# Step orders of their own for the first three and the last four periods of a software-pipelined FP32 transformer kernel

## The chip, the cores and the metric

One core of one Trainium2 chip. The metric is the device time of one execution in microseconds (us), where lower is better. Every run quoted here was in the fast state, and all kernels gave correct results. PE is TensorE, PEld its weight loads, DVE VectorE, ACT ScalarE, POOL GpSimd and SP SyncE, which issues the large DMA transfers.

## The reference

128 batch items of S = 128 tokens with E = 512 features go through two layers, all in FP32: attention with 8 heads, whose scores are multiplied by twice the adjacency matrix, then a graph attention layer. Both are pre-normalised and residual.

```python
h = jnp.maximum(_layernorm(x, axis=-1), 0.0)
# layer 0
q, k, v = (proj(Wq, bq), proj(Wk, bk), proj(Wv, bv))         # proj: x @ W.T + b, 8 heads
scores = jnp.einsum('bhqd,bhkd->bhqk', q, k) * SCALE * (adj + adj)[:, None]
ctx = jnp.einsum('bhqk,bhkd->bhqd', softmax(scores), v)
x = x + jnp.einsum('bse,fe->bsf', ctx, Wo) + bo
# layer 1
h = jnp.maximum(_layernorm(x, axis=-1), 0.0)
Wh = h @ W
e = leaky_relu(Wh @ a[:512] + swapaxes(Wh @ a[512:], 1, 2), 0.2)
attention = softmax(where(adj > 0.5, e, -9e15), axis=1)
x = x + elu(attention @ Wh)
```

## The kernel before

The items are worked in N = 64 pairs, two pairs making a group. A 512x512 product is made from seven products of quarters (as in Strassen's method), some with *sums* of quarters of the weights (`weight_sums`, four additions on DVE) or of the activations (`hidden_sum`, four additions per group). A group has 21 such products (v0 to v6, q0 to q6, k0 to k6). Each is 4 matmuls, which the trace lists as 8 records of 128x256. Their results stand in PSUM banks "a", "b" and "c". ACT copies out the first one of a quadrant ("firsts"), DVE adds the others ("adds").

```python
SEQ = "v0 v1 v2 v3 v4 q0 v5 q1 v6 q2 q3 q4 k0 q5 k1 q6 k2 k3 k4 k5 k6".split()
N = B // 2                                                    # 64 pairs

def weight_sums(w):
    nc.vector.tensor_tensor(w[:, 4], w[:, 1], w[:, 0], OP.subtract)
    nc.vector.tensor_tensor(w[:, 5], w[:, 3], w[:, 4], OP.subtract)
    nc.vector.tensor_tensor(w[:, 1], w[:, 3], w[:, 1], OP.subtract)
    nc.vector.tensor_tensor(w[:, 6], w[:, 2], w[:, 5], OP.subtract)
```

All work of a pair is cut into steps with short names, and one list, `ORDER`, says in which order they are written in one period: "U4:0" is step U4 of this period's pair, "fb:4" step fb of the pair four before. There is no scheduler behind it (`manual_schedule`): the list is each engine's program. The names used below: U1 to U11 the products of the *next* group (U1 to U10 with the even pair of a group, the rest of SEQ with the odd one), F their firsts, A their adds, sca/scb the scores of a pair's two items, at, mx, ex, rc, nm their weighing and softmax, fl, bl, pl the transposition of the attention (on DVE, then through DRAM), pc the context product, o0 to o6 the output products of layer 0, d00 to d11 the dot products of layer 1, g its gather, w0 to w6 its output products, fa, fb, so the finish and the store.

Group 0 has no earlier pair that it could stand beside. It is straight-line code, and what is needed once hangs on the first use, as whole calls:

```python
    with tc.manual_schedule():
        ...                                # stats and transposes of pairs 0 and 1
        weight_sums(wv_sb)
        ...
        for n, u in enumerate(SEQ):
            firsts, adds = product(0, u[0], int(u[1]))
            if n == 2:
                weight_sums(wq_sb)
            ...                            # stats of pairs 2 and 3, sums of wk, sums of group 1
            firsts()
            adds()
        ...
        first_use = {
            (0, "mxa"): constant_c, (0, "mxb"): lambda: weight_sums(wo_sb), (0, "atb"): constant_u,
            (0, "st0"): spread_u, (1, "mxa"): lambda: weight_sums(w1_sb),
        }
        for p in range(early, N + late):   # -22 .. 91: periods at both ends are partly empty
            for step, lag in ORDER:
                pair = p - lag
                for do in tables.get(pair, {}).get(step), first_use.get((pair, step)):
                    if do:
                        do()
```

`constant_u` is eight dot products on DVE in one piece. At the end the periods simply run empty: there is no next group, so the U steps are missing and the rest stays in the same order.

Of the kernel before, what the change touches and what calls it, by code (L numbers as in the profile page):

```python
# [13 lines left out]
P = 128  # L14
# [10 lines left out]
def kernel(  # L25
# [40 lines left out]
    def load_x(p):  # L66

        xs[p] = io.tile([P, 2, E], F32, name="x")
        if p < 2:
            for i in range(2):  # L70
                nc.sync.dma_start(xs[p][:, i, :], x[2 * p + i])
        else:
            nc.sync.dma_start(xs[p], both(x, p))
# [6 lines left out]
    def half_of_hidden(p):  # L80

        g, i = divmod(p, 2)
        if i == 0:
            hAs[g] = grp.tile([P, 4, 2, 2 * S], F32, name="hA")
        return hAs[g][:, 2 * i : 2 * i + 2].rearrange("p q c k -> p (q c) k")

# [10 lines left out]
        adjTs[p] = aio.tile([P, 2, S], F32, name="adjT")  # L97
        nc.sync.dma_start(adjTs[p], both(adjT, p))

    load_x(0)  # L100
    load_x(1)

    ident = const.tile([P, P], F32, name="ident")
    make_identity(nc, ident)
    mhalf = const.tile([P, 1], F32, name="mhalf")
    nc.gpsimd.memset(mhalf, -0.5)

    def quarters(src, name):

        w = const.tile([P, 7, 2, E // 2], F32, name=name)  # L110
        nc.sync.dma_start(w[:, 0:4], src)
        return w

    def column(src, name):
        b = const.tile([P, C], F32, name=name)
# [1 line left out]
            nc.scalar.dma_start(b, src.rearrange("(c p) -> p c", p=P))  # L117
        return b

    def row(src, offset, name):  # L120
        b = const.tile([P, E], F32, name=name)
        nc.sync.dma_start(b, bass.AP(tensor=src.tensor, offset=src.offset + offset, ap=[[0, P], [1, E]]))
        return b

    bq_sb = column(bq, "bq")
    bk_sb = column(bk, "bk")
    bv_sb = column(bv, "bv")
    wv_sb = quarters(wvT, "wv")
    wq_sb = quarters(wqT, "wq")
    load_x(2)  # L130
    load_x0(3)
    wk_sb = quarters(wkT, "wk")
    load_adj(0)
    wo_sb = quarters(woT, "wo")
    c_sb = row(bo, 0, "c")
    w1_sb = quarters(w1, "w1")
    us_sb = row(a1, 0, "u_src")
    ut_sb = row(a1, E, "u_dst")



# [4 lines left out]
    FIRSTS = {0: (0, 0), 2: (1, 0), 4: (1, 1), 5: (0, 1)}  # L146
    ADDS = {1: (0, 0, "b"), 4: (1, 1, "c"), 6: (1, 0, "c")}

    def weight_sums(w):
        nc.vector.tensor_tensor(w[:, 4], w[:, 1], w[:, 0], OP.subtract)  # L150
        nc.vector.tensor_tensor(w[:, 5], w[:, 3], w[:, 4], OP.subtract)
        nc.vector.tensor_tensor(w[:, 1], w[:, 3], w[:, 1], OP.subtract)
        nc.vector.tensor_tensor(w[:, 6], w[:, 2], w[:, 5], OP.subtract)

    def token_sum(h, s, k):

# [22 lines left out]
        return mv, stats, power  # L179

    st0, rows0, qks, vs, scs, ats, trs, blocks, aTs, pcs = ({} for _ in range(10))
    l1s, h1s, wts, pbs, pgs, gTs, zs, ezs, posts = ({} for _ in range(9))

    def stats0(p, i, src=None):
        if p not in st0:
            st0[p] = row_stats(x0s.pop(p) if src is None else src, "mv0")
        st0[p][1](i)

    def hidden_T(p, src, tag):

        mv, _, power = st0.pop(p)
        power()
        dst = half_of_hidden(p)
        hn = work.tile([P, 2, E], F32, name="hn", tag=tag)
        for i in range(2):
            nc.vector.tensor_scalar(
                hn[:, i, :], src[:, i, :], mv[:, i, 0:1], mv[:, i, 1:2], op0=OP.subtract, op1=OP.mult
            )
        for i in range(2):
            pt = ps1.tile([P, C, P], F32, name="pt", tag="ps1")  # L200
            for c in range(C):
                nc.tensor.transpose(pt[:, c, :], hn[:, i, c * P : (c + 1) * P], ident)  # L202
            nc.scalar.activation(dst[:, :, i * S : (i + 1) * S], pt, AF.Relu)

    def spread0(p):

        mv, _, power = st0.pop(p)
        power()
        rows0[p] = dram.tile([2, P, 2], F32, name="rows0")
        with nc.allow_non_contiguous_dma(reason="two numbers of a row"):  # L210
            nc.gpsimd.dma_start(rows0[p].rearrange("b p s -> p b s"), mv)
# [285 lines left out]

    ucol = const.tile([P, 2, C], F32, name="ucol")

    def constant_c():  # L500

        pm = ps1.tile([P, 2, E // 2], F32, name="pm", tag="ps1")
        for f in range(2):
            for c in range(C):
                nc.tensor.matmul(
                    pm[:, f, :], bv_sb[:, c : c + 1].to_broadcast([P, P]), wo_sb[:, 2 * (c // 2) + f, c % 2, :],
                    start=(c == 0), stop=(c == C - 1),
                )
        nc.vector.scalar_tensor_tensor(c_sb, pm.rearrange("p f k -> p (f k)"), -1.0, c_sb, op0=OP.add, op1=OP.add)

    def constant_u():

        junk = work.tile([P, E], F32, name="junk")
        for i, u in ((0, us_sb), (1, ut_sb)):
            for c in range(C):
                k = c // 2
                nc.vector.scalar_tensor_tensor(  # L517
                    junk.rearrange("p (f k) -> p f k", f=2), w1_sb[:, 2 * k : 2 * k + 2, c % 2, :], 1.0,
                    u.rearrange("p (f k) -> p f k", f=2), op0=OP.mult, op1=OP.mult, accum_out=ucol[:, i, c : c + 1],
                )  # L520

    def spread_u():

        for i, u in ((0, us_sb), (1, ut_sb)):
            pu = ps1.tile([P, C, P], F32, name="pu", tag="ps1")
            for c in range(C):
                nc.tensor.transpose(pu[:, c, :], ucol[:, i, c : c + 1].to_broadcast([P, P]), ident)
            nc.scalar.activation(u, pu.rearrange("p c k -> p (c k)"), AF.Copy, scale=1.0 if i else 1.0 / MASK)


    SEQ = "v0 v1 v2 v3 v4 q0 v5 q1 v6 q2 q3 q4 k0 q5 k1 q6 k2 k3 k4 k5 k6".split()
# [1 line left out]



    ORDER = [
        (step.split(":")[0], int(step.split(":")[1]))
        for step in """
        F4:1 F6:1 flb:1 fb:4 U9:1 F9:1 g1:3 od5:2 ge1:3 o6:2 la:1 st0:2 s0:1 hd0:1 od6:2 U8:1 w0:3 st1:2 gs0:3 blb:1
        hd1:1 pw:2 w1:3 gs1:3 nm:2 U10:1 zc0:3 so:4 U1:0 gs2:3 h20:2 A9:1 A8:1 l0:0 wd1:3 w2:3 F10:1 gs3:3 h21:2 plb:1  # L540
        lx:1 hs0:1 zc2:3 lT:0 sca:0 pca:1 pcb:1 scb:0 w4:3 d00:2 d01:2 pea:1 A6:1 ata:0 mxa:0 peb:1 d10:2 w3:3 F1:0
# [2 lines left out]
        zc5:3 atb:0 F2:0 mxb:0 F3:0 o2:1 e1:2 A10:16 cs3:1 wd6:3 U5:0 F5:0 sw:2 exb0:0 A2:0 U4:0 exb2:0 A3:28 exb3:0  # L544
        exb1:0 A5:0 A11:1 bla:0 o3:1 rcb1:0 od2:1 nmb2:0 U6:0 hs3:1 o4:1 lt:0 rcb0:0 nmb0:0 t0:0 nmb3:0 nmb1:0 pla:0
        U7:0 ez:3 F7:0 F11:-22 g0:2 fa:3 od4:1 A1:15 od4c:1 ge0:2 o5:1 A7:14
        """.split()
    ]

    def steps(p):  # L550

        a, b = 2 * p, 2 * p + 1
        table = {}
        for s, n in (("a", a), ("b", b)):
            table |= {
                "sc" + s: lambda n=n: scores(n),
                "at" + s: lambda n=n: weigh(n),
                "mx" + s: lambda n=n: maxima(n),
                "fl" + s: lambda n=n: flip_blocks(n),
                "bl" + s: lambda n=n: send_blocks(n),  # L560
                "pl" + s: lambda n=n: place_blocks(n),
                "pc" + s: lambda n=n: context(n),
                "pe" + s: lambda n=n: keep_context(n),
            }
            for k in range(4):
                table[f"ex{s}{k}"] = lambda n=n, k=k: exps(n, k)
                table[f"nm{s}{k}"] = lambda n=n, k=k: normalise(n, k)
            for k in range(2):
                table[f"rc{s}{k}"] = lambda n=n, k=k: shares(n, k)
# [23 lines left out]
            "ez": lambda: elu(p), "fa": lambda: finish_a(p), "fb": lambda: finish_b(p), "so": lambda: store(p),  # L593
            "sh": lambda: shift(p),
        }
        if p > 2:
            table["lx"] = lambda: load_x(p)
        if p + 1 < N:
            table["la"] = lambda: load_adj(p + 1)
        if p + 4 < N:  # L600
# [22 lines left out]
        return table  # L623

    with tc.manual_schedule():
        def first_stats(p):
            stats0(p, 0, rows[p])
            stats0(p, 1)

        rows = [xs[0], xs[1], xs[2], x0s[3]]  # L630
        first_stats(0)
        first_stats(1)
        hidden_T(0, rows[0], "h2")
        hidden_T(1, rows[1], "z")
        weight_sums(wv_sb)
        for k in range(4):
            hidden_sum(0, k)
        for n, u in enumerate(SEQ):
            firsts, adds = product(0, u[0], int(u[1]))
            if n == 2:  # L640
                weight_sums(wq_sb)
            if n == 4:
                first_stats(2)
            if n == 6:
                hidden_T(2, rows[2], "h2")
            if n == 8:
                weight_sums(wk_sb)
            if n == 10:
                first_stats(3)
            if n == 12:  # L650
                hidden_T(3, rows[3], "z")
                load_x0(4)
            if n == 14:
                for k in range(4):
                    hidden_sum(1, k)
            firsts()
            adds()
        stats0(4, 0)
        stats0(4, 1)
        spread0(4)  # L660

        early, late = min(lag for _, lag in ORDER), max(lag for _, lag in ORDER)
        tables = {p: steps(p) for p in range(N)}

        first_use = {
            (0, "mxa"): constant_c, (0, "mxb"): lambda: weight_sums(wo_sb), (0, "atb"): constant_u,
            (0, "st0"): spread_u, (1, "mxa"): lambda: weight_sums(w1_sb),
        }
        for p in range(early, N + late):
            for step, lag in ORDER:  # L670
                pair = p - lag
                for do in tables.get(pair, {}).get(step), first_use.get((pair, step)):
                    if do:
                        do()


# [40 lines left out]
```

## Time and profile before

| | before |
|---|---|
| device time, median of 3 | 2416.63 us (2416.42 to 2416.77) |
| span of the profiled execution | 2412.4 us |
| PE busy / idle in it | 2366.6 / 45.8 us |

To read it: PE is the bound, so only two things can shorten the span. One is PE's *idle* time, 45.8 us. The other is the *slow* part of its busy time: the granted clock (the share of TensorE's full speed that it is allowed to run at) falls to half after some gaps, and the same matmuls are then busy for longer. The number of PE records is the same in every kernel below except two, where it is told. So less busy time means less work at half clock. The views are in the prediction.

### The profile page before, as it was taken

What the parts mean: (1) busy time and instruction counts of PE and PEld (TensorE: products, weight loads), DVE (VectorE), ACT (ScalarE), POOL (GpSimd) and SP (SyncE); (2) the same over time, 40 slices, a digit from 0 to 9 for tenths busy, and PEclk for the clock granted to TensorE, in tenths of its full rate; (3) what the DMA queues carried; (4) which work ended last, traced back from release to release, by engine and by line L of the source; (5) the groups of instructions that cost most, each with busy time, mean ns of one, the idle gap of its engine ahead of it and who ended that gap; (6) DMA issues with size and microseconds to landing.
All of it is one profiled execution on the core that took longest, in us unless ns stands there. A gap on an engine that the chain in (4) does not pass through costs nothing.

```text
span 2412.4 us, 40507 instructions
## 1 busy us (share of the span) xinstructions
PE 2366.6 (98%) x14264; PEld 2072.9 (86%) x14264; DVE 1993.3 (83%) x3909; ACT 1460.3 (61%) x4811; POOL 265.7 (11%) x323
## 2 busy tenths in 40 slices
PE   8899999999999999999999999999999999999987
PEld 7788888888888888888888888888888888888875
DVE  5788888888888888888888888888888888888776
ACT  2565666665666665656655656656666656666664
POOL 1011111111101101111111111111011011010000
PEclk9999999999999999999999999999999999999998
DMA  4434534544434545445445345455345454454232
GB/s 164 114 106 127 147 112 124 157 114 136 134 114 134 148 122 138 113 124 146 133 127 146 104 121 158 115 135 138 113 131 158 114 136 124 120 138 133 82 106 72
DMA packets 255275, 306.10 MB, mean 127 GB/s; under 512 B 21856, under 2 KB 181600, under 8 KB 254432
## 3 DMA queue, kind: packets, MB, share of 16 engines
q1 hardware_dynamic: 251568, 303.37, 45.0%
q8 instruction: 113, 1.85, 0.3%
q0 software_dynamic: 1920, 0.13, 0.2%
q14 instruction: 90, 0.74, 0.1%
q10 hardware_dynamic: 1584, 0.01, 0.0%
HBM read 202.64 MB, written 100.79 MB: 126 GB/s over the span
## 4 chain that ended last, share of the span: by engine, by line
PE 96%; DVE 2%; ACT 1%; DMA 1%; issue 0%; SPq 0%; POOL 0%; POOLq 0%; ACTq 0%; DVEq 0%
PE acc_a L261 27%; PE row_a L302 23%; PE acc_c L261 13%; PE row_c L302 9%; PE acc_b L261 7%; PE sc L323 6%; PE pc L386 5%; PE pg L464 5%; PE pb L432 1%; ACT at L341 0%; ACT at L350 0%; PE pt L202 0%; DVE junk L517 0%; DVE tr L357 0%; DVE at L329 0%
## 5 line engine op out<-in xcount | busy, mean ns | idle before, releaser
L341 ACT ACTIVATE at<-at,nmx 128x128 f32<-128x128 f32 x1024 | 397.1, 393 | 17.4 <-DVE nmx L336 16.4
L302 PE MATMUL row_a<-w,gT 128*128 128x256 f32 x1280 | 326.1, 385 | 7.7 <-DVE z L482 6.8
L302 PE MATMUL row_a<-wo,cxT 128*128 128x256 f32 x1280 | 322.3, 383 | 9.3 <-DVE x L400 9.3
L350 ACT ACTIVATE at<-at,rs 128x128 f32<-128x128 f32 x1024 | 316.5, 389 | 13.7 <-DVE rs L345 13.7
L176 POOL TENSOR_SCALAR mv<-mv 128x2 f32<-128x2 f32 x128 | 78.4, 613 | 2090.7 <-DVE mv L173 2090.7
L302 PEld LDWEIGHTS row_a<-w,gT 128*128 128x128 f32 x1280 | 237.9, 190 | 47.4 <-DVE z L482 8.4
L478 ACT COPY z<-row_a 128x256 f32<-128x256 f32 x256 | 92.8, 362 | 305.2 <-PE row_a L302 305.1
L302 PEld LDWEIGHTS row_a<-wo,cxT 128*128 128x128 f32 x1280 | 235.6, 192 | 37.3 <-DVE x L400 10.1
L329 DVE SCALAR_TENSOR_TENSOR at<-sc,adj 128x1024 f32<-128x1024 f32 x128 | 156.7, 1225 | 94.8 <-PE sc L323 92.6
L278 ACT ACTIVATE kT<-acc_a,bk 128x256 f32<-128x256 f32 x256 | 107.5, 471 | 162.2 <-PE acc_a L261 162.2
L341 ACT ACTIVATION_READ_ACCUMULATOR at<-at,nmx 128x1 f32 x1024 | 195.8, 191 | 0.0
L357 DVE STREAM_TRANSPOSE tr<-at 128x1024 f32<-128x1024 f32 x128 | 158.7, 1240 | 38.2 <-ACT at L350 37.5
L172 DVE BATCH_NORM_STATS2 st<-x 128x6 f32<-128x512 f32 x256 | 175.2, 685 | 8.8 <-DMA x<-in_x 4.3
L400 DVE TENSOR_TENSOR x<-row_a,x 128x256 f32<-128x256 f32 x320 | 132.6, 414 | 48.0 <-PE row_a L302 45.6
L273 ACT COPY v<-acc_a 128x512 f32<-128x512 f32 x128 | 74.8, 585 | 154.5 <-PE acc_a L261 154.5
L336 DVE TENSOR_REDUCE nmx<-at 128x8 f32<-128x1024 f32 x128 | 156.2, 1220 | 4.4
L393 ACT COPY cxT<-pc 128x512 f32<-128x512 f32 x128 | 75.0, 586 | 136.5 <-PE pc L386 136.5
L323 PEld LDWEIGHTS sc<-kT,qT 64*128 64x128 f32 x2048 | 125.6, 189 | 33.5 <-issue 31.8
L323 PE MATMUL sc<-kT,qT 64*128 64x128 f32 x2048 | 150.3, 287 | 1.3 <-DVE at L329 1.3
L464 PEld LDWEIGHTS pg<-w,h 128*128 128x128 f32 x1024 | 136.2, 194 | 8.6 <-ACT w L452 1.8
L177 POOL TENSOR_TENSOR mv<-mv,mhalf 128x2 f32<-128x2 f32 x128 | 140.6, 1099 | 10.7
L464 PE MATMUL pg<-w,h 128*128 128x128 f32 x1024 | 136.6, 277 | 1.4 <-DVE w L458 1.4
(126 smaller groups left out, 4995.0 us busy)
## 6 DMA issues: line engine op xcount, KB each, us to landing
blocks<-tr SPq DMA_DIRECT2D x128, 512.0 KB, 4.6
aT<-blocks SPq DMA_DIRECT2D x512, 128.0 KB, 3.0
x<-in_x SPq DMA_DIRECT2D x123, 512.0 KB, 5.3
out<-x SPq DMA_DIRECT2D x64, 512.0 KB, 5.0
hA<-in_xT SPq DMA_DIRECT2D x120, 256.0 KB, 4.5
mr<-rows SPq DMA_DIRECT2D x60, 256.0 KB, 5.0
adj<-in_adj SPq DMA_DIRECT2D x64, 128.0 KB, 2.9
adjT<-in_adjT SPq DMA_DIRECT2D x64, 128.0 KB, 3.4
```

Of the source, the lines that this page charges most:

```text
L172: nc.vector.bn_stats(st, src[:, i, :])
L177: nc.gpsimd.tensor_tensor(mv[:, :, 1], mv[:, :, 1], mhalf.to_broadcast([P, 2]), OP.pow)
L261: nc.tensor.matmul(acc[:, m, :], lhsT, rhs, start=fresh and m == 0 and c == 0, stop=c == 1, skip_group_check=True)
L302: nc.tensor.matmul(acc, left[:, la, c, :], w[:, wb, c, :], start=n in (0, 3) and c == 0, stop=c == 1, skip_group_check=True)
L323: nc.tensor.matmul(sc[:, s * C + j, :], qT[r, j, cols], kT[r, j, cols], start=True, stop=True)
L329: nc.vector.scalar_tensor_tensor(at, scs.pop(b), QSCALE, adjs[p][:, i : i + 1, :].to_broadcast([P, H, S]), op0=OP.mult, op1=OP.mult)
L336: nc.vector.tensor_reduce(nmx, at, AX.X, OP.max, negate=True)
L341: nc.scalar.activation(at[:, j, :], at[:, j, :], AF.Exp, bias=nmx[:, j : j + 1], accum_out=sums[:, j : j + 1])
L350: nc.scalar.activation(at[:, j, :], at[:, j, :], AF.Copy, scale=rs[:, j : j + 1])
L357: nc.vector.transpose(trs[b], at.rearrange("p h (j k) -> p j h k", k=Q))
L400: nc.vector.tensor_tensor(d, row_acc(p, "o", bank), d, OP.add)
L464: nc.tensor.matmul(pg[:, c, :], h1s[p][0][:, i, c * P : (c + 1) * P], wts[p][:, i, :], start=True, stop=True)
```

## The change

The intent is to fill the two ends. The middle list stays, but only for periods 3 to 59. Two explicit lists take the rest: `HEAD` (group 0 with the loads, the weights' sums and the periods 0 to 2) and `TAIL` (the last four periods, pairs counted from the end). For this, what were whole calls become single steps: `W{v,q,k,o,w}{0..3}` for the weights' sums, `cu00` to `cu11` for the dot products of `constant_u`, `sup`, `sua`, `ccp`, `ccd` for the other constants, `L...` for loads. No arithmetic comes or goes.

```diff
-    def weight_sums(w):
+    def weight_sum(w, k):
         ...                                        # one of the four subtractions
-    def constant_u():
+    def dots_u(i, half):                           # two of the eight dot products
+    HEAD = """
+        lx@0 t0@-5 Lu0@0 t1@-5 lt@0 Lq@0 Lk@0 pp@0 lx@1 hn0@0 hn1@0 tp0@0 Wq0@0 Lu1@0 t1@-4 t0@-4 tp1@0 pp@1 Wq2@0 hn0@1
+        ev0@0 Lv@0 ev1@0 U3@-1 U5@-1 Wk0@0 U1@-2 lx@2 hn1@1 F1@-2 tp1@1 Lo@0 tp0@1 Wq1@0 la@-1 Lw@0 ev0@1 la@0 ev1@1
+        ...                                        # 372 steps in all
+    """
     ORDER = ...                                    # unchanged
+    TAIL = """
+        ...
+        U2@-4 nma2@-2 pcb@-3 m1@-5 scb@-2 st0@-4 pea@-3 od6@-4 st1@-4 fla@-2 e1@-5 A9@-3 so@-6 sw@-5 peb@-3 o0@-3 g1@-5
+        ...                                        # 598 steps in all
+    """
-        first_use = { ... }
-        for p in range(early, N + late):
+        for step, p in HEAD:
+            do(step, p)
+        for p in range(EARLY, N - LATE):           # 3 .. 59
             for step, lag in ORDER:
-                ...
+                if p >= lag:
+                    do(step, p - lag)
+        for step, p in TAIL:
+            do(step, N + p)
```

In `HEAD` the products of group 0 are U1 to U10 of "pair" -2 and U1 to U11 of "pair" -1. The list starts with k0 and k1 (U3 and U5 of -1), which need no sums. In `TAIL` the last group's v products (U1 to U5, U7, U9 of pair -4) stand scattered among the steps of the last pairs.

## The prediction

> **What bounds the kernel now.** I read the page first, then the busy time of each engine by stretch of the span, then PE's waits in the two stretches that were not full, then the clock around one gap. The page:
>
> ```profile
> PE 2366.6 (98%) x14264; PEld 2072.9 (86%) x14264; DVE 1993.3 (83%) x3909; ACT 1460.3 (61%) x4811; POOL 265.7 (11%) x323
> ...
> PE   8899999999999999999999999999999999999987
> ...
> PEclk9999999999999999999999999999999999999998
> ```
>
> PE is busy 98% of the span, and only the first two and last two slices are below full. Busy time by stretch (start:end, length, then busy us of PE, PEld, DVE, ACT, POOL, granted clock, DMA share, GB/s):
>
> ```profile
> 0.00:12.00 12.00, 3.50 (x17) 3.46 (x18) 6.78 (x15) 3.07 (x4) 2.94 (x11) 1.00 0.80 282
> 12.00:120.00 108.00, 96.22 (x496) 81.95 (x496) 70.28 (x125) 44.91 (x145) 8.91 (x15) 0.95 0.39 124
> 120.00:2320.00 2200.00, 2200.00 (x13401) 1932.28 (x13400) 1850.62 (x3633) 1369.20 (x4534) 250.57 (x291) 1.00 0.46 128
> 2320.00:2412.40 92.40, 66.85 (x356) 55.19 (x354) 65.61 (x139) 43.12 (x129) 3.27 (x6) 0.87 0.28 90
> 2236.00:2382.40 146.40, 133.28 (x821) 115.76 (x821) 114.46 (x235) 88.39 (x295) 4.36 (x8) 0.94 0.31 94
> 2382.40:2412.40 30.00, 17.58 (x75) 13.02 (x74) 15.71 (x35) 9.22 (x20) 1.09 (x2) 0.88 0.13 49
> ```
>
> From 120 to 2320 us PE has no gap and full clock: nothing can be won there by order alone. The head loses 120 - 3.50 - 96.22 = 20.3 us of PE, the tail 92.40 - 66.85 = 25.6. PE's waits in the first 120 us, then in the last 93 (what waited, for what: total, times, longest):
>
> ```profile
> PE pt L202 <- DVE hn L196: 8.9, 2, 8.5
> PE acc_c L261 <- DVE v L282: 5.5, 1, 5.5
> PE pc L386 <- DMA aT<-blocks: 2.4, 1, 2.4
> PE sc L323 <- DVE at L329: 1.3, 1, 1.3
> PE acc_a L261 <- ACT v L273: 1.2, 1, 1.2
> PE acc_a L261 <- ACT kT L278: 0.9, 1, 0.9
> ```
>
> ```profile
> PE row_a L302 <- DVE x L400: 9.3, 2, 5.5
> PE row_a L302 <- DVE z L482: 6.8, 4, 1.9
> PE pg L464 <- DVE w L458: 1.4, 1, 1.4
> PE row_a L302 <- ACT z L478: 0.9, 2, 0.5
> ```
>
> The gaps have a second price. The 5.5 us wait ends at 78.4, and the clock around it is:
>
> ```profile
> 76.00:78.00 2.00, 0.00 (x0) 0.00 (x0) 2.00 (x4) 2.00 (x11) 0.00 (x0) 0.79 0.00 0
> 78.00:80.00 2.00, 1.56 (x4) 1.29 (x5) 1.29 (x5) 1.74 (x8) 0.49 (x2) 0.50 0.00 0
> 82.00:84.00 2.00, 2.00 (x6) 1.62 (x5) 1.97 (x3) 0.15 (x1) 0.00 (x0) 0.50 0.50 183
> 84.00:86.00 2.00, 2.00 (x10) 1.77 (x10) 1.79 (x3) 0.00 (x0) 0.00 (x0) 1.00 0.99 140
> ```
>
> For about 6 us PE ran at half clock. Summing busy time times lost clock over 2 us stretches: head 5.56 x 0.5 (78 to 84) + 4.0 x 0.43 (94 to 98) = 4.5 us; tail, after its gaps of 3.8, 1.9, 5.5, 1.9 and 1.9 us, about 1.7 + 1.7 + 2.7 + 1.7 + 1.7 = 9.5. The first 16 transposes took 3.67 us where 16 records run in 1.74, 1.9 more. **Lost: head 20.3 + 4.5 + 1.9 = 26.7 us, tail 25.6 + 9.5 = 35.** All else, about 2412.4 - 62 = 2350 us, is PE work that the change does not touch.
>
> **What the skill says.** "TensorE: Matmul & The Clock Gate", section "Why this matters for your kernels": no PE-idle gaps over about 3 us between bursts, else the clock drops to 4/8. The trace agrees (0.50 after 5.5 us), and is stricter: in the tail 1.9 us gaps were followed by 0.50 too. The same page, "Architectural detail", calls ACT and DVE strict FIFO: so the place of a step in one engine's list decides, and a blocked step blocks all behind it. The 5.5 us wait is that: two additions to v needed about 0.7 us each, but stood in DVE's list behind eight dot products for u (67.7 to 73.5) and the sums of wo (74.6 to 77.2). "DMA: Bandwidth & Descriptors", section "Where 436 GB/s comes from", gives a ceiling of 435 GB/s; the trace shows 400 to 436 GB/s from 6 to 22 us, so early loads queue for bandwidth. "Perfetto Trace Analysis", "Identifying the Most-Contended Engine", warns that matmul busy share is a bad measure; so I count records per time (8 of 128x256 in 1.73 us at full clock), not the share.
>
> **The change part by part.** No arithmetic goes or comes (the same products, sums, stats); the periods between keep their order. Three things move.
>
> *Start, a small loss.* Before: x of pairs 0 and 1, then wv, then wq. After: x of pair 0, two small loads, wq, wk, x of pair 1, a small one, wv. The first two products are k's first two, with raw quarters of the weights and pair 0 alone. They need 0.5 + 0.25 + 0.125 + 2 = 2.9 MB; integrating the GB/s of the old trace, 2.9 MB have moved by 10.7 us, and loads were seen to land about 1 us behind: 11.8. Two products of 1.73 last to 15.3. The third needs wv, 4.7 MB in, about 16.2: a gap of 0.9. So six products and the 16 transposes are done at 16.2 + 4 x 1.73 + 0.9 = 24.0; the old kernel had seven by 24.2. This part costs about 1.6 us.
>
> *Rest of the head, the gain.* The old kernel loses 26.7 - 8.7 (start) - 1.9 = 16 us after 24 us. The new list scatters the sums of wo and w1 and the dot products among the additions, starts the first scores after 17 products (old: 20 of group 0 and one of group 1), and mixes group 0's with group 1's products. Going through it: between the first scores and the first context product stand 16 products, 27.6 us, plus 3; the chain there is at 1.24 + maximum 1.22 + exponentials 3 + scaling 2.45 + transpose 1.25 + blocks out and in 9.6 (82.25 to about 92), some 19 us. The second half of the pair goes through the one at buffer after it, 12 us later, so that context product may still wait 0 to 2 us. DVE has 98 us of work beside 110 of PE in this list (counts times durations), so it can keep up. I leave 3 us of gaps: gain 16 - 3 - 1.6, about **11 to 12 us**.
>
> *Tail.* The old tail drops to pairs without products of a next group, which are bound by DVE's chain: PE waits for x (3.8 and 5.5 us) twice per the last pairs. The new list holds back the last group's v products (and some of q and k) until 54 to 84 us of PE work before the end, as filler. From 2236 on the old trace has 114.46 + 15.71 = 130 us of DVE work; PE's is 133.28 + 17.58 less 9.5 of slow clock = 141. The end chain, after the last output product of the last pair, was 30.0 us: stats to last dot product 7.0, 1.9 behind w products until the transposes of the scores, softmax 3.65, gather and w products 9.9, finish and store 7.4. The new order puts those transposes ahead; with a better clock I get about 27 us, with 15 us of PE work in it: 12 lost. Before it PE has 126 us and DVE 130 - 16 = 114; that is 90% for DVE, where the steady part has 84% and the best 20 us show 96%. I allow 5 us of gaps and 2 of slow clock. Lost: 12 + 5 + 2 = 19 instead of 35: gain **16 us**.
>
> Sum: 28 us, 2416.6 - 28 = **2388 us**.
>
> **Rivals.** *The lists are fitted to wrong durations*: a DVE step stands ahead of something late and blocks. Speaks for it: 970 steps with no slack rule, and DMA time, which varies (blocks 4.6, aT 3.0 us). Against: the middle list of the same kind runs 2200 us without a gap. It would leave 10 to 15 us of gain: 2402 to 2407. *DVE becomes the bound of the tail*: the filler raises DVE's needed share to 90%; if it stays at 84%, the 114 us take 136 and another 5 us go: 2393. *Everything fits*: head gaps 0, tail only the end chain: 12 + 12 lost instead of 62, 2378 to 2380. *Weights come too late*: each us that wq, wk and wv are later is a us at the start; 5 us at worst: 2393.
>
> **Range and chances.** The best case bounds the gain at about 38 us, 1.6%; 2% is 48 us, more than head and tail can give with the start (12) and the end chain (12) left. Getting slower by 2% would need the new lists to add 48 us of gaps in some 230 us. So range 2378 to 2401, chances 0.015, 0.97, 0.015.
>
> **What would show it.** Right: PE full from about 24 us on, clock 1.00 at 80 to 100 us, no 5.5 us wait for v, first product near 12 us with a short wait at the third; PE full until about 30 us before the end, the waits for x gone or under 2 us, DVE busy at 90% in the last 150 us; middle unchanged. Wrong: PE waits over 3 us in the head (a DMA or v, x, kT additions), half clock in the tail as before, or first matmuls after 15 us.

## The result, and the profile after

The changed kernel took 2380.25 us (median of 5, 2378.95 to 2381.24) against 2416.42 (5 runs, 2411.46 to 2416.77). The ratio is 0.9856 (95% interval 0.9841 to 0.987). A ratio here is the mean time of one kernel's fast runs over the mean of the other's fast runs of the same rounds, so not quite the ratio of the medians. The gain of 1.4% is inside the 2% that counts as the same, and inside the predicted range: 8 us under the predicted 2388, and 2 us above the range's lower end.

The interval of a ratio is 0.001 to 0.0015 to either side. So a gain against the kernel before is known to about 3 us, and a difference between two changed kernels, which is taken below over two such ratios, to 4 or 5 us.

The page of the changed kernel (busy time, then forty slices of the span in tenths):

```profile
PE 2355.3 (99%) x14264; PEld 2062.0 (87%) x14264; DVE 1988.5 (84%) x3909; ACT 1457.4 (61%) x4811; POOL 265.7 (11%) x323
...
PE   8999999999999999999999999999999999999998
PEclk9999999999999999999999999999999999999999
```

The span went from 2412.4 to 2377.1, by 35.3 us. PE's busy time fell by 11.3 with the same 14264 records; that is work which no longer ran at half clock. Idle time fell by 24.0, from 45.8 to 21.8. Where the rest of the idle time lies is shown by the busy times by stretch after (columns as in the prediction):

```profile
0.00:12.00 12.00, 1.97 (x8) 1.57 (x8) 3.45 (x7) 2.48 (x3) 1.64 (x9) 1.00 0.73 253
12.00:24.00 12.00, 10.84 (x47) 9.39 (x48) 7.75 (x16) 2.40 (x5) 2.20 (x4) 1.00 1.03 413
24.00:120.00 96.00, 96.00 (x565) 83.19 (x564) 78.49 (x143) 53.79 (x186) 8.61 (x13) 1.00 0.34 100
2200.00:2347.00 147.00, 146.46 (x906) 125.03 (x905) 124.56 (x259) 99.18 (x335) 4.80 (x10) 1.00 0.39 116
2347.00:2377.20 30.20, 20.00 (x102) 15.67 (x100) 20.08 (x43) 11.09 (x23) 1.89 (x2) 0.96 0.14 53
```

PE is full from 24 us on, and up to 2347 it lost 0.54 us. What is left is the start, with 24 - 1.97 - 10.84 = 11.2 us, and the chain after the last pair's layer 0, with 30.2 - 20.0 = 10.2. PE's longest waits of the whole run after (total, times, longest) say the same:

```profile
PE pt L189 <- DVE hn L182: 7.3, 1, 7.3
PE acc_a L250 <- DMA wk<-in_wkT: 3.9, 1, 3.9
PE row_a L291 <- DVE z L471: 1.7, 1, 1.7
PE row_a L291 <- ACT z L467: 1.2, 3, 0.5
```

Every wait of the old list is gone except the first one, for the first x and its normalisation, and the layer 1 chain. One wait is new, for wk. The start of PE's timeline after (start, length, engine, line, what, in brackets the idle time before it):

```profile
7.26 1.97 PE L189 MATMUL pt<-ident,hn 128*128 128x128 f32 x8 [7.26 <-DVE hn L182]
13.16 3.53 PE L250 MATMUL acc_a<-hA,wk 128*128 128x256 f32 x8 [3.94 <-DMA wk<-in_wkT]
16.53 1.89 PE L250 MATMUL acc_b<-hA,wk 128*128 128x256 f32 x8
```

The first product started at 13.16, and it ran at half speed: 3.53 us for what the next one did in 1.89. The granted clock of these stretches reads 1.00 all the same, but that reading says nothing: the trace file has no clock record before 16.3 us, and the view prints 1.00 where there is none. The first record, of full speed, starts at 16.3 us, as the first product ends. (In all ten traces a stretch at half clock lasts 3.41 or 6.83 us, save those that the program's end cuts off.)

### The profile page after: what moved, and what is told of

Same layout as the page of the kernel before. It is cut to its first block, busy times and chain, and to the rows that moved or that the text cites. A ratio compares the mean times of both kernels' runs of the same rounds, so it can differ in the third digit from the quotient of the medians.

```text
span 2377.1 us, 40536 instructions
## 1 busy us (share of the span) xinstructions
PE 2355.3 (99%) x14264; PEld 2062.0 (87%) x14264; DVE 1988.5 (84%) x3909; ACT 1457.4 (61%) x4811; POOL 265.7 (11%) x323
## 4 chain that ended last, share of the span: by engine, by line
PE 99%; DMA 1%; DVE 0%; ACT 0%; issue 0%; DVEq 0%
PE acc_a L250 28%; PE row_a L291 24%; PE acc_c L250 14%; PE row_c L291 9%; PE acc_b L250 7%; PE sc L312 6%; PE pc L375 5%; PE pg L453 5%; PE pb L421 1%; DMA wk<-in_wkT 0%; PE pm L494 0%; DMA bq<-in_bq 0%; PE pt L189 0%; DVE junk L412 0%; DVE x L479 0%
## 5 line engine op out<-in xcount | busy, mean ns | idle before, releaser
L160 DVE BATCH_NORM_STATS2 st<-x 128x6 f32<-128x512 f32 x256 | 175.3, 685 | 10.9 <-DMA x<-in_x 6.7
```

Source lines behind the costliest of these rows:

```text
L160: nc.vector.bn_stats(st, src[:, i, :])
```

## The experiments

**1. The new head alone, and 2. the new tail alone.** *head_only* keeps `HEAD` and lets the old list run to the end:

```diff
-        for p in range(EARLY, N - LATE):
+        for p in range(EARLY, N + 28):
             ...
-        for step, p in TAIL:
-            do(step, N + p)
```

*tail_only* keeps `TAIL` and writes the old head's steps, one for one, into `HEAD`. I compared the order of the instructions with the kernel before on every engine: it is the same up to period 60.

```diff
     HEAD = """
-        lx@0 t0@-5 Lu0@0 t1@-5 lt@0 Lq@0 Lk@0 pp@0 lx@1 ...
+        lx@0 lx@1 Lv@0 Lq@0 lx@2 l0@-2 Lk@0 la@-1 Lo@0 Lc@0 Lw@0 Lu0@0 Lu1@0 t0@-5 t1@-5 t0@-4 t1@-4 pp@0 ...
```

> The new head with the old periods' order to the very end (the old tail). If head and tail are separate and additive, as I hold, the head is worth what the two traces show up to a common point: PE is full and at full clock from 17 us on in the changed kernel, so it has lost about 13 us by 120 us where the old one lost 27: a gain of about 14 us, and the last 92 us look as in the kernel before (waits of PE for x of 3.8 and 5.5 us, clock near 0.87). Rival: the middle gained too because the new head left it in a better state; then the gain is over 20 us and the tail differs.

> The old head, step for step, then the periods' order, then the new tail. Additive theory: a gain of about 21 to 22 us (36 less 14), the first 120 us as before with the 5.5 us wait for v and half clock after it, the last 150 us with no PE wait over 2 us. Rival, that the tail's list needs the state that the new head leaves: less than 15 us.

head_only took 2402.08 us (2397.31 to 2403.03, 5 runs) and tail_only 2394.48 (2393.07 to 2395.6, 5 runs), against 2414.84 before on the same chip. The ratios are 0.9943 (0.993 to 0.9955) and 0.9916 (0.9903 to 0.993), which is 13.8 and 20.3 us. Together that is 34.1, where the whole change gave 0.0144 x 2414.84 = 34.8, as two independent ends would. The traces show it more sharply. From its 1,000th to its 13,000th record PE has the same work in the same order in all these kernels. The changed kernel reaches the 2,000th record 13.8 us before the old one (head_only 12.9). From there to the 12,000th all four kernels take 1646.2 us. The rest takes the changed kernel and tail_only 382.0 us, the old kernel 403.6 and head_only 402.8. The profiled executions split each gain:

| kernel | span | PE busy | PE idle | against before: idle, half clock |
|---|---|---|---|---|
| before | 2412.4 | 2366.6 | 45.8 | |
| head_only | 2398.7 | 2362.3 | 36.4 | -9.4, -4.3 |
| tail_only | 2391.7 | 2360.3 | 31.4 | -14.4, -6.3 |
| after | 2377.1 | 2355.3 | 21.8 | -24.0, -11.3 |

In head_only the old end is back, with its waits for x and its lower clock (busy by stretch, then waits):

```profile
2300.00:2398.80 98.80, 72.86 (x389) 60.22 (x388) 71.23 (x154) 50.22 (x160) 3.27 (x6) 0.87 0.26 84
```

```profile
PE row_a L291 <- DVE x L389: 9.3, 2, 5.5
PE row_a L291 <- DVE z L471: 7.0, 4, 2.2
```

In tail_only the old head is back (clock 0.95, 11.8 us of idle PE), and the new end behaves as in the changed kernel, with 20.03 us of PE work in the last 30.2:

```profile
12.00:120.00 108.00, 96.19 (x495) 81.93 (x494) 69.95 (x125) 44.49 (x145) 8.89 (x15) 0.95 0.40 123
...
2361.60:2391.80 30.20, 20.03 (x102) 15.70 (x100) 20.10 (x43) 11.09 (x23) 1.89 (x2) 0.95 0.14 53
```

**3. Is the head's order needed, or just a new list?** *block* is the changed kernel with the eight dot products and the four sums of wo put back in one piece each:

```diff
     HEAD = """
-    ... F3@-2 cu01@0 F2@-1 U4@-1 F9@-1 tp1@2 cu00@0 U8@-1 ...          # also cu10, cu11, Wo0 to Wo3 taken from their places
+    ... fla@0 atb@0 cu00@0 cu01@0 cu10@0 cu11@0 U10@0 mxb@0 Wo0@0 Wo1@0 Wo2@0 Wo3@0 U6@-1 ...
```

(sup0 stands two small steps later than in the changed kernel.)

> The changed kernel with one thing of the old head put back: VectorE's dot products for u stand together behind the second scores' product with adj of pair 0, and the four sums of wo together behind its maxima, as in the old list (8.3 us of VectorE work in one place); all else is left. If a step's place in VectorE's strict list is what made PE wait 5.5 us for v in the old kernel, PE waits again for an addition of v, q or k by 3 to 6 us near 60 to 75 us, runs at half clock after it, and the whole is 4 to 9 us slower than the changed kernel. Rival: the new list has PE work in hand there (27 us of products between the scores and the context product), and hides the block: under 2 us.

2388.62 us (2387.91 to 2388.7, 4 runs), ratio 0.9892 (0.9877 to 0.9907). The changed kernel has 0.9856, so this costs 0.0036 x 2413 = 8.7 us, near the top of the expectation; PE's wait, 6.5 us, is a little above the 3 to 6 expected. PE's timeline and the clock around the new wait:

```profile
70.76 3.37 PE L250 MATMUL acc_b<-wv,hA 128*128 128x256 f32 x8 [6.46 <-DVE kT L271]
```

```profile
66.00:68.00 2.00, 0.00 (x0) 0.00 (x0) 1.97 (x4) 1.72 (x9) 0.00 (x0) 0.69 0.07 24
...
70.00:72.00 2.00, 1.24 (x3) 1.06 (x4) 1.97 (x6) 1.18 (x4) 0.23 (x2) 0.50 0.00 0
```

This is the old 5.5 us wait again, on another addition (kT in place of v): PE stands 6.5 us while DVE is full, and then runs at half clock. So small work that stands in DVE's list in one block, and not scattered, costs more than half of the head's gain. In the trace it is 7.4 us by the 2,000th PE record. Another 1.5 us came at the very end, by chance as far as the traces tell: a gap of 1.68 us in the chain of layer 1, which eight of the ten traces have, was followed by half clock in this one alone.

**4. Is the filler what the tail needed?** *no_filler* is the changed kernel with the v products of the last group (and their firsts and adds) all together ahead of the scores of pair 62, not scattered:

```diff
     TAIL = """
-    ... nma1@-2 U1@-4 U2@-4 nma2@-2 ... o1@-3 F1@-4 ge0@-5 ... U3@-4 ... F3@-4 ... U5@-4 ... U4@-4 ... U7@-4 ... U9@-4 ...
+    ... U4@-3 F4@-3 U1@-3 U1@-4 F1@-4 U2@-4 A2@-4 U3@-4 F3@-4 U4@-4 U5@-4 F5@-4 A5@-4 U7@-4 F7@-4 U9@-4 A9@-4 sca@-2 ...
```

> The changed kernel with one thing undone in the tail: the seven products for v of the last group, with their copies and additions, stand together before the scores of the last pair but one, not spread over the next 40 us of PE work. If the held-back products are what fills PE there, 12 us of PE work are missing later and PE waits for x and z again: 6 to 12 us slower than the changed kernel. Rival: what fills the tail is the interleaving of the four pairs' own steps, and the products' place hardly matters: under 3 us.

2390.96 us (2389.29 to 2392.7, 4 runs), ratio 0.9901 (0.9888 to 0.9915), 10.9 us slower than the changed kernel. The same ten microseconds of the changed kernel, and then of no_filler with a later stretch:

```profile
2270.00:2280.00 10.00, 10.00 (x68) 8.20 (x67) 7.69 (x13) 5.01 (x19) 0.00 (x0) 1.00 0.32 107
```

```profile
2270.00:2280.00 10.00, 9.60 (x45) 8.11 (x43) 0.69 (x1) 1.65 (x4) 0.00 (x0) 1.00 0.00 0
...
2320.00:2330.00 10.00, 5.72 (x25) 4.74 (x26) 8.38 (x23) 6.75 (x21) 1.89 (x2) 0.75 0.31 73
```

While the products stand together, PE is nearly full but DVE has 0.69 us of work where it had 7.69. DVE's work of the last pairs is not done earlier; it is pushed behind. Fifty microseconds later DVE is the one that is busy, and PE has 5.72 us in ten and a clock of 0.75. PE waits again, though not for x and z, as expected, but for the softmax weights and the gathered rows of layer 1:

```profile
PE pg L453 <- DVE w L447: 3.5, 2, 2.0
PE row_a L291 <- ACT gT L459: 3.5, 1, 3.5
```

The filler is not extra work: it is PE work kept for when DVE would otherwise be alone. One thing the run does not separate. The additions to v moved together with the products, and DVE stood in its list before two of them for 5.6 and 5.0 us. So it shows that the products' place matters, but not how much of the loss is PE work missing later and how much is DVE held up at that place.

**5. How much room does the middle have?** *late_dve* puts twelve useless additions ahead of one step in three middle periods:

```diff
             for step, lag in ORDER:
+                if p in (20, 30, 40) and step == "wm":
+                    for _ in range(12):
+                        idle = work.tile([P, E], F32, name="junk")
+                        nc.vector.tensor_tensor(idle, us_sb, ut_sb, OP.add)
```

> The price of one gap by itself: in periods 20, 30 and 40 of the changed kernel, where PE is full, VectorE gets twelve needless additions (12 x 0.61 = 7.3 us) ahead of the mask of the second layer. The result stays right. If gaps cost twice, by the wait and by the half clock after it, each of the three places shows a PE wait of w and then some 6 us at a lower clock, and the total grows by 3 x (w + about 3 us); with w of 3 to 5 us that is 18 to 24 us. Rival, that only the wait counts: growth equal to the sum of the PE waits. If PE has enough work in hand to cover 7.3 us of VectorE, no growth at all.

2408.57 us (2407.02 to 2409.32, 8 runs), ratio 0.9975 (0.9965 to 0.9985): 0.0119 x 2413 = 28.7 us slower than the changed kernel, more than expected. One of the three places in the timeline, DVE's and then PE's row:

```profile
770.06 8.67 DVE L721 TENSOR_TENSOR junk<-u_src,u_dst 128x512 f32<-128x512 f32 x12
...
779.12 3.78 PE L250 MATMUL acc_b<-wv,hA 128*128 128x256 f32 x8 [7.40 <-DVE w L427]
```

The block was 8.67 us long (0.72 an addition, where I had counted with 0.61), and PE waited 7.4 us, so the list has about 1.3 us of room at this place. The three waits together:

```profile
PE acc_b L250 <- DVE w L427: 22.2, 3, 7.4
```

The product after each gap ran at half speed: 3.78 us in place of 1.89. From the 2,000th to the 12,000th PE record this kernel takes 29.55 us longer than the changed one. Less the waits that leaves 7.4 us, about 2.5 for each gap. (PE's busy time over the whole run rose by 8.9, 2364.2 against 2355.3, but 1.5 of that lies before the 2,000th record, in a start that was slow for longer.) Here nothing but DVE's list differs, so the price of a gap of this size is its length and some 2.5 us more.

**6. The start: 6a. the loads in another order.** *loads_first* is the changed kernel with wk and wv, which the first three products need, ahead of wq and of the small loads:

```diff
     HEAD = """
-        lx@0 t0@-5 Lu0@0 t1@-5 lt@0 Lq@0 Lk@0 pp@0 lx@1 hn0@0 ... Lu1@0 ... Lv@0 ... lx@2 ...
+        lx@0 t0@-5 t1@-5 Lk@0 lx@1 Lv@0 Lq@0 lx@2 Lu0@0 Lu1@0 lt@0 pp@0 hn0@0 hn1@0 ...
```

(Wq0 then stands ahead of Wq1, and Wq2 behind Wk3, since wq comes later.)

> The changed kernel with only its first loads in another order: x of pair 0, wk, x of pair 1, wv, wq, x of pair 2, and the small rows after them; on VectorE two sums of wq stand later. My theory: in the changed kernel the first product waits 3.9 us for wk, which is issued third and lands at 13.0 us; with 1.5 MB ahead of it instead of 2.9, wk lands before 10 us, the first product starts at 9.5 to 10.5 us and the whole gains 2 to 3 us over the changed kernel (about 2377.5 us). Rival: the start is free because PE waits later for x of pair 1 or wq anyway; then the same time and a new PE wait before 25 us.

2376.7 us (2376.53 to 2377.46, 4 runs), ratio 0.9843 (0.9829 to 0.9856), by the ratios 3.1 us faster than the changed kernel. That is within the noise of two ratios, but the traces bear it out: PE's 2,000th record comes 2.3 us earlier than in the changed kernel, and 2.5 to 3.2 earlier than in head_only, no_filler and late_dve, which have the same start. PE's timeline:

```profile
10.72 3.63 PE L250 MATMUL acc_a<-hA,wk 128*128 128x256 f32 x8 [0.69 <-ACT hA L192]
```

The first product came 2.4 us earlier than in the changed kernel (1.6 to 1.9 earlier than in head_only, block, no_filler and late_dve), waits for ACT and not for wk, and no later wait appeared. But it still takes 3.63 us.

**6b and 6c. Warming the clock.** *warm* adds 26 transposes of the identity ahead of the first real ones in the same PSUM tile, *warm_through* 34 and another 6 between the transposes and the first product (so these two have 14290 and 14304 PE records). Both start from loads_first.

```diff
     def turn_hidden(p, i):
         pts[p, i] = ps1.tile([P, C, P], F32, name="pt", tag="ps1")
+        if (p, i) == (0, 0):
+            for k in range(34):                    # warm: 26
+                nc.tensor.transpose(pts[p, i][:, k % C, :], ident, ident)
     ...
         acc = accs[g, which, bank]
+        if (g, which, n) == (0, "k", 0):           # warm_through alone
+            for k in range(6):
+                nc.tensor.transpose(acc[:, 0, :P], ident, ident)
```

> The other order of loads (the run loads_first) and, ahead of the first real transposes, 26 transposes of the identity into the same PSUM tile, whose result is overwritten. In both kernels the first work of PE ran at half speed (8 records of 128x256 in 3.5 us, 8 transposes in 1.97 us) though the profile shows a granted clock of 1.00. If PE was at half clock from standing idle, it now runs them in 1.73 and about 0.9 us, and the whole gains 2 to 3 us over loads_first (about 2374 us). Rival: the slow start is the loads that run beside it, or the operands that come late; then the first product still takes 3.5 us and nothing is gained.

> As the run warm, but with 34 idle transposes ahead of the first real ones and 6 more between them and k's first product (into its accumulator, which that product's first matmul clears), so that PE has no gap of a microsecond before that product. In the run warm the real transposes ran at full speed (8 in 1.1 us), but the clock was back at 0.50 from 9.9 to 13.1 us after gaps of 1.1 and 0.7 us. If those gaps closed it, k's first product now takes 1.73 us instead of 3.5 and the whole gains 1.7 us over warm (about 2374 us). Rival: transposes don't count as work for the clock; then the product is as slow as before, and the whole the same or up to 0.5 us slower.

warm: 2375.64 us (2373.99 to 2376.8, 4 runs), ratio 0.9838 (0.9824 to 0.9851), about 1.2 us faster than loads_first, less than expected and within the noise. The real transposes took 1.11 us for eight in place of 1.97. But there was a gap of 1.1 us before them and one of 0.7 after them, and the clock fell back before the first product (its stretch, then its row):

```profile
10.00:11.00 1.00, 1.00 (x3) 0.82 (x4) 0.67 (x1) 0.00 (x0) 0.00 (x0) 0.50 0.99 410
...
9.72 3.67 PE L253 MATMUL acc_a<-hA,wk 128*128 128x256 f32 x8 [0.72 <-ACT hA L195]
```

warm_through closes the gaps. 2375.0 us (2374.21 to 2375.42, 5 runs) against 2416.0 (9 runs), ratio 0.9833 (0.982 to 0.9846). Its timeline:

```profile
1.35 6.61 PE L190 MATMUL pt<-ident 128*128 128x128 f32 x34 [1.35 <-POOL ident masks.py:199]
...
9.82 1.99 PE L256 MATMUL acc_a<-hA,wk 128*128 128x256 f32 x8
...
2336.87 1.09 PE L381 MATMUL pc<-aT,v 128*64 128x128 f32 x16 [1.73 <-DMA aT<-blocks]
```

The first product now runs at full clock, 1.99 us in place of 3.67. That is the 1.7 us expected: PE's 2,000th record of the common work comes 1.6 us earlier than in warm and 2.5 earlier than in loads_first. In the profiled execution a wait of 1.73 us in the tail takes most of it back. On SP's list the load of the last x stands ahead of the reads of the last attention blocks; that load waited 2.6 us for the store which has to empty its buffer (0.4 in loads_first). The profiled run is the slowest of the five, 2375.42; whether the others, down to 2374.21, have that wait can't be told without their traces. I left it there: moving the load behind the reads would make x itself late, and what is at stake is under 0.1%. warm_through is the fastest version measured, but its interval overlaps those of warm and loads_first.

## Why the prediction was right

The mechanism held: nothing came from the middle, the gain came from gaps and from the half clock that followed them, and the two ends add up. The sizes held less well: 28 us were predicted, 35 came, because the reserves for gaps were hardly needed, while the start cost more than booked. So errors of opposite sign partly cancel in the sum. The terms:

- **The middle, unchanged.** Right: 120 to 2320 was full before, 24 to 2347 lost 0.54 us after, and the same 10,000 PE records take 1646.2 us in both.
- **Head, "11 to 12 us".** Measured alone 13.8. The "3 us of gaps" that were left for the rest of the head were 0: no PE wait over 0.4 us between 24 and 120. The context product that "may still wait 0 to 2 us" didn't wait. That 5.5 us wait for v as a step in DVE's list blocked by small work was right, shown by block.
- **Start, "costs about 1.6 us".** Mis-sized. wk was put at 11.8 and landed at 13.0 (+1.3 for the first product's start). I had integrated the transfer rates of the *old* trace, 282 GB/s over the first 12 us, and this execution moved 253. But much of that is chance: in head_only, block, no_filler and late_dve, with the same start, the first 12 us moved 274 to 278 GB/s, PE waited 2.7 to 2.9 us for wk, and the first product started at 12.3 to 12.6. loads_first, which takes wq and three small loads from before wk and wv, recovered some 3 us; how much of that is wq and how much the small loads was not separated. The first product was counted at 1.73 us and took 3.53 (+1.6 against a warm first product's 1.99, shown by warm_through). In the old kernel 16 transposes in a row came first and the product after them took 2.07 us, so they had warmed the clock; I had booked their slowness as lost time without asking who pays it in the new order. In return, the gap of 0.9 at the third product did not come. Six products were done at 26.0, not 24.0. The start cost 3.6 by this count and the rest of the head gave 16, which makes 12.4; the other 1.4 of the measured 13.8 is not accounted for. The start alone differs by about 1 us from execution to execution (the 2,000th PE record came 12.9 to 13.8 us before the old kernel's in the four traces with the new head unchanged), and in the five traces with this order of loads the first record of full clock starts anywhere from 15.6 to 18.7 us.
- **Tail, "16 us".** Measured alone 20.3. "5 us of gaps" before the end chain were 0.54 and "2 of slow clock" none: the clock is 1.00 up to the last matmul, and the 0.96 of the last stretch comes from the empty end (in this trace: the same end chain did fall to half clock in block). The end chain was put at 27 us with 12 lost; it is 28.7 long but has 10.2 us of idle PE, since more of the layer 1 products fall into it. Against this, the old half clock was overrated: 9.5 us by 2 us stretches, where tail_only's busy time shows 6.3 regained.
- **DVE at 90%.** In the 126 us that this figure is for, 2221 to 2347, DVE is busy 109.8 us, 87%, and PE isn't held. So the rival "DVE becomes the bound of the tail" (2393) is out. no_filler shows what a tail that waits costs: 10.9 us, when the filler doesn't stand where DVE needs time.
- **"Lists fitted to wrong durations" (2402 to 2407).** Out: no wait in either list but those of the start and of the end chain. That such a list breaks easily is shown by block and late_dve, with 8.7 us and 28.7 us for three blocks.
- **"Weights come too late".** The one rival that came true in part: 3.9 us of wait for wk in this execution, 2.7 to 2.9 in the others, and some 3 us could be had back. With it came one of the signs that the prediction had named for being wrong, a PE wait over 3 us in the head for a DMA. The total survived it because the 3 us left for other gaps in the head were not used.
- **"Everything fits" (2378 to 2380).** The nearest of all. I had given up 10 us for gaps (3 + 5 + 2) because it seemed unlikely that 970 steps fit; but the same procedure had already made a middle list without a gap, and that was the better evidence.

The last question is whether a gap's second price was real. The clock rows around block's wait, and the time that late_dve lost beyond its waits, say yes: about 2.5 us on top of a gap of 7.4. The Trainium skill, "TensorE: Matmul & The Clock Gate", section "What's actually happening", says that the throttled state is the default and that activity releases it. This case's first product agrees, with 3.53 us cold and 1.99 after 48 transposes (40 of them of the identity).

## What to carry to other kernels

A pipelined loop that is full in the middle still loses at both ends, where its order was made for neighbours that aren't there. Write the ends as lists of their own, cut one-time work into single steps, and keep some independent PE work back for the last stages. When you count such a gain, count each gap on the bound engine with its length *and* the slow clock that may follow it, and at the start ask what the first matmul after a quiet time will cost. Judge whether a fitted list will hold by how well lists of the same origin hold elsewhere in the kernel.

## What the Trainium skill lacked or had wrong

- "TensorE: Matmul & The Clock Gate", "Part 4: PE-mode transpose", says that transposes don't count as PE-busy the same way and that the full clock doesn't engage for them. Here they warmed the clock: after 26 transposes of the identity (5.46 us from a cold start) eight real ones took 1.11 us, where cold ones take 1.97, and the trace's first record of full clock starts at 6.3 us, when PE had run nothing else. With 40 transposes ahead and no gap, the first product ran at full speed (1.99 us against 3.63 in loads_first).
- The same page, "Why this matters for your kernels", asks for no gaps over about 3 us. Shorter ones already brought the half clock: 1.1 and 0.7 us close together in warm, 1.9 us in the old tail (all three). And the length alone does not decide: the gap of 1.68 us in the new end chain brought it in one of eight traces.
- No page read here measures what one gap costs in a kernel that is otherwise full: for 7.4 us, about 2.5 us more at half clock (late_dve, 7.4 us for three).
- No page read here says that a trace can have no clock record while PE is still cold: the changed kernel's first one starts at 16.3 us, and the view prints 1.00 before it, while eight records take 3.53 us that take 1.89 later.
- "DMA: Bandwidth & Descriptors", "Where 436 GB/s comes from", gives 435 GB/s as the ceiling of the fabric, which the prediction used, but says that loads from HBM are bound by about 358. Here, with one core at work, the loads moved 413 GB/s from 12 to 24 us, so the higher figure is the nearer one. Neither can be used for the first microseconds: the first 12 us moved 253 to 282 GB/s, and the order of the first loads alone shifted the first product by 1.6 to 2.4 us (loads_first).
